# Sorted prefix sums in place of a dense attention, on 14 of 32 samples of a four-layer graph network

## The chip, the cores and the metric

The kernel runs on one core of a Trainium2 chip. The metric is the device time of one execution in microseconds (us), as the median of a few runs; a profile of one further execution is read beside it. Engines: PE (TensorE, matrix products and transposes), DVE (VectorE), ACT (ScalarE), POOL (GpSimd), SP (the queue that issues most DMAs). Each engine runs its own instructions in order and waits on semaphores for the others.

## The reference

32 samples of 512 nodes with 256 features go through four layers, each `x = x + layer(relu(layernorm(x)))`. Layers 0, 2 and 3 are attentions over a given graph `adj`. Layer 1 is a small network with two graph attentions; its first one has no mask, so every node attends to every node:

```python
out = relu(x @ mlp1_w + mlp1_b)            # 512 x 512
h  = out @ W_fc                            # 512 x 512
f1, f2 = h @ a[:512], h @ a[512:]          # one number per node each
e   = leaky_relu(f1[i] + f2[j], 0.2)
att = softmax(e, over j)
out = elu(elu(att @ h)) + residual         # then mlp2_w, and a second, masked attention
```

`leaky_relu` has two straight pieces. For a fixed i, all j with f2[j] above -f1[i] take the weight exp(f1[i] + f2[j]), the others exp(0.2 (f1[i] + f2[j])). Each weight is a factor of i times a factor of j. With the nodes sorted by f2, a row of `att @ h` is a sum over a tail of the sorted nodes with one factor, and over the head with the other.

## The kernel before

Everything is fp32. A sample is held as 4 tiles of 128 nodes or as 512-wide feature-major blocks of 128 partitions. `pipelined` (L597) does not emit instructions at once: the layer functions record them in a `Plan` (L82), which knows for each instruction what it reads and writes (`add`, L124), a cost by engine (`cost`, L333) and which rotating buffer it takes: 60 blocks of 128x512 in SBUF, 8 PSUM banks, small tiles. `order` (L169) then lays all 32 samples out as one list, instruction by instruction: it takes the one that can start first, and among equals the one with the earliest due time, which is the sample's number times PERIOD, less the longest chain of costs behind it, less a hand-set number in URGENT (keys like "p0:0", tile name and layer). STARTS, PACE and LAYERS hold layers back until a set time; OWN, SPARE and KEEP keep buffers for older samples; AHEAD limits how many samples are in flight; SWITCH prices a change of PE between full products, products tiled by columns and products tiled by rows. `issue` (L281) emits the list; all planned instructions have line L297.

The first attention of layer 1 is `first_gat` (L803). PE computes h = o1 W_fc for nodes (mm<-W_fc,o) and the two numbers f1, f2 per node (sd). `largest` finds the largest f2, `on_all` (L756) puts a vector on all partitions by four transposes. DVE makes four 128x512 tiles p of unnormalised weights, one `tensor_scalar` each with two factors per partition and a maximum. `inverse_sums` (L774) adds the four, transposes the total, reduces it and spreads the reciprocals by four more transposes. `weighted` multiplies: 4 feature blocks by 4 node blocks, 16 products of 128x128 by 128x512 (av<-p,v 128*128 128x512). `elu2` (L789) scales by the reciprocals, applies the two elus and adds the residual, on ACT and DVE.

Around it, the other layers do their masked attentions: scores with pairs of 64-row products (sc<-qT,kT, layer 0), products tiled by columns (64 or 32 columns) for av and for sums, exponentials on ACT (p<-R,e; p<-sc), masks on DVE. SP's queue carries R<-rd (a row of scores spread over 128 partitions), the round trip of sums and reciprocals through DRAM (s<-sums, few<-s, s<-few, rc<-s) and x in and out. POOL computes the layernorm's power (rs) and issues accumulating DMAs (p<-p in layer 3, x<-boa in layer 0). The masks of layers 0 and 1 are bf16, that of layer 3 is f32. If tests on the data at the end fail (`tests`, L992, flag go), a slower `general` path (L1086) computes everything again.

Of the kernel before, what the change touches and what calls it, by code (L numbers as in the profile page):

```python
# [12 lines left out]
F32 = mybir.dt.float32  # L13
BF16 = mybir.dt.bfloat16
I32 = mybir.dt.int32
AF = mybir.ActivationFunctionType
# [25 lines left out]

PERIOD = 107.0
STARTS, PACE = (0.0, 4.0, 19.0, 123.0), 101.0
LAYERS = (0.0, 32.0, 34.0, 184.0)

URGENT = {
    "stats:0": -231, "mv:0": -37, "rs:0": -123, "ms:0": -205, "h:0": 11, "pt:0": -750, "hT:0": 14, "mm:0": -216,  # L50
    "sc:0": -122, "p0:0": -65, "total:0": -98, "av:0": 34, "sums:0": -578, "s1:0": 49, "few:0": -6, "s2:0": 16,
    "rc:0": -235, "oT:0": 85, "mv:1": -1, "rs:1": -312, "ms:1": 79, "h:1": -294, "pt:1": -8, "hT:1": 210, "o1:1": 230,
    "sd:1": -3, "v1:1": 496, "nd:1": -243, "ew:1": 150, "p1:1": 192, "total:1": -170, "sm:1": 80, "rs1:1": -271,
    "rc:1": 295, "av:1": -43, "y:1": -155, "e:1": -181, "o2:1": 223, "o3:1": 97, "v2:1": -74, "sd2:1": 230,
    "mn:1": -599, "None:1": 532, "ew2:1": 73, "p2:1": 326, "rs2:1": -12, "u:1": 67, "x:1": 261, "stats:2": 253,
    "mv:2": -2, "ve:2": -111, "rs:2": 9, "ms:2": 327, "h:2": -217, "pt:2": 246, "hT:2": -176, "mm:2": -27,
    "vs:2": -140, "es4:2": -547, "e4:2": 121, "rd:2": -46, "R:2": 10, "p3:2": -509, "av:2": -104, "total:2": -557,
    "sm:2": 273, "r4:2": -73, "ue:2": -350, "x:2": -11, "stats:3": -7, "mv:3": -124, "ve:3": 186, "rs:3": 271,
    "ms:3": -493, "pt:3": 488, "hT:3": -507, "mm:3": -191, "vs:3": -282, "es8:3": 187, "e8:3": -10, "rT:3": -676,
    "rd:3": 450, "R:3": 367, "p3:3": -733, "av:3": -428, "total:3": 545, "sm:3": -50, "sums:3": 213, "raw:3": 11,  # L60
    "s1:3": 84, "s2:3": 121, "rc:3": -208, "oT:3": 42, "None:3": 359, "af:3": 10, "top:3": 409, "ok:3": 38,
    "values:3": -217, "rows:3": 208, "gp:3": -60, "gram:3": -190, "gab:3": 123, "sq:3": -31, "tp:3": -40,
    "res:3": 224,
# [18 lines left out]
class Plan:  # L82
# [9 lines left out]
    HOP, AHEAD = 0.05, 4  # L92

    OWN = dict(block=8, bank=2)
    SPARE = dict(block=2, bank=1)

# [27 lines left out]
    def add(self, attribute, engine, op, args, kw):  # L124
        steps = self.samples[-1]
        out = kw["out"] if "out" in kw else args[0]
        busy, lasts = cost(engine, op, args, kw, out)
        step = self.joined or Step(engine, busy)
        if not step.calls:
            step.layer = self.layer  # L130
            steps.append(step)
        step.calls.append((attribute, op, args, kw))
        step.urgent = URGENT.get(f"{self.kinds.get(out.tensor.name)}:{step.layer}", 0.0)
        step.lasts = step.busy + lasts
        writes = [out] + ([kw["accum_out"]] if "accum_out" in kw else [])
        reads = [v for v in list(args) + list(kw.values()) if isinstance(v, bass.AP) and not any(v is w for w in writes)]
        for ap, writing in [(v, False) for v in reads] + [(v, True) for v in writes]:
            if ap.tensor.name not in self.tile_tag:
                continue
            name, box = ap.tensor.name, extent(ap)  # L140
            if name not in step.touches:
                step.touches.append(name)
            record = self.history.setdefault(name, [])
            for other, obox, owriting in record:
                bank = writing and owriting and step.engine == other.engine == "PE"
                if (writing or owriting) and other is not step and (bank or overlap(box, obox)):
                    if other not in step.before:
                        step.before.append(other)
                        other.after.append(step)
            record.append((step, box, writing))  # L150
        for other in self.gate:
            if other not in step.before:
                step.before.append(other)
                other.after.append(step)
        self.gate = []

    def behind(self, ap):

        self.gate = [step for step, _, writing in self.history[ap.tensor.name] if writing]
# [9 lines left out]
    def order(self):  # L169
# [17 lines left out]
        free["block"][:FILLED] = [FILLED_TO] * FILLED  # L187
# [14 lines left out]
        result, count, mode = [], sum(map(len, self.samples)), "full"  # L202
        oldest = 0

        def slots(step):

            when, taken = 0.0, {}
            for name in step.touches:
# [17 lines left out]
                when = max(when, sorted(free[tag])[n])  # L226
# [3 lines left out]
        while len(result) < count:  # L230
            best = None
            for engine, waiting in open_.items():
                for step in waiting:
                    if step.sample > oldest + self.AHEAD:
                        continue
                    start = max(at[engine], step.ready)
                    if engine == "PE" and step.mode != mode:
                        start = max(start, at[engine] + self.SWITCH[mode])
                    if best is not None and self.key(start, step) >= best[0]:
                        continue  # L240
                    when = slots(step)
                    if when is None:
                        continue
                    start = max(start, when)
                    if best is None or self.key(start, step) < best[0]:
                        best = self.key(start, step), start, step
            assert best is not None, "the buffers do not suffice"
            _, start, step = best
            step.start = start
            open_[step.engine].remove(step)  # L250
# [3 lines left out]
            end = start + step.lasts  # L254
            for name in step.touches:
                tag, s = self.tile_tag[name], step.sample
                if name not in live:
                    live.add(name)
                    free[tag].remove(min(free[tag]))
# [21 lines left out]
    def issue(self, tc, late):  # L281
# [3 lines left out]
        for layer in range(3):  # L285
# [5 lines left out]
            begin = first  # L291
        with tc.manual_schedule():
            for n, step in enumerate(steps):
                for f in at.get(n, ()):
                    f()
                for attribute, op, args, kw in step.calls:
                    getattr(getattr(self.nc, attribute), op)(*args, **kw)  # L297
# [35 lines left out]
def cost(engine, op, args, kw, out):  # L333
# [15 lines left out]
    if engine == "DVE":  # L349
# [5 lines left out]
        return 0.066 + 0.00105 * n + (0.06 if by_pointer else 0.0), 0.085  # L355
    if engine == "POOL":
        if op == "dma_start":
            return 1.1, (5.2 if n == N else 8.0)
        return (1.0 if n < 16 else 0.683), 0.1
    size = 4  # L360
    for _, k in (out.ap if out.tensor.name.startswith(("few", "R", "rc", "x")) else src.ap):
        size *= k
    return 0.4, 3.4 + size / 190e3
# [3 lines left out]
def gnn_stack_kernel(ctx: ExitStack, tc: tile.TileContext, a: dict, out: bass.AP):  # L367
# [45 lines left out]
    go1 = const.tile([1, 1], F32, name="go1")  # L413

    spread = const.tile([P, B], F32, name="spread")
    bq8 = const.tile([P, KD], F32, name="bq8")
# [11 lines left out]
    mask0T = const.tile([P, NT, N], BF16, name="mask0T")  # L428
    mask1T = const.tile([P, NT, N], BF16, name="mask1T")
# [4 lines left out]
    def new_x():  # L434
        return first.tile([P, NT, D], F32, name="x", bufs=5)
# [4 lines left out]
    with prep_stack, tc.manual_schedule():  # L440
# [21 lines left out]
        nc.vector.memset(ones, 1.0)  # L462
        adjf = prep.tile([P, NT, N], F32, name="adjf", bufs=1)
# [133 lines left out]
    def pipelined(stack):  # L597
# [3 lines left out]
        dram = stack.enter_context(tc.tile_pool(name="dram", bufs=6, space=bass.MemoryType.DRAM))  # L601
        q = Plan(nc, PERIOD)
        def block(name):

            return q.tile(big, [P, N], name, BLOCKS, keep=KEEP, tag="block")
# [7 lines left out]
        def small(name, *free):  # L613
            return q.tile(big, [P, *free], name, 4)

# [212 lines left out]

        def second_gat(o3, xt):

            v, sd = q.tile(big, [P, NT, D + 1], "v2", 2), small("sd2", NT, 2)
            for t in range(NT):
                ps = node_major(wh, t, o3, 0, D + 2)
                q.scalar.activation(v[:, t, :D], ps[:, :D], AF.Identity, bias=ones[:, 0:1])
                q.scalar.copy(sd[:, t, :], ps[:, D : D + 2])
            q.vector.memset(v[:, :, D : D + 1], 1.0)
# [13 lines left out]
            for t in range(0, NT, 2):  # L850
                e, u, avs, rs = block("e"), block("u"), [], small("rs2", 2, 2)
                for i in range(2):
                    av = bank("av")
                    avs.append(av)
                    for j in range(NT):
                        q.tensor.matmul(
                            av[:, : D + 1], p[j][:, col(t + i)], v[:, j, :], start=(j == 0), stop=(j == NT - 1)
# [23 lines left out]
        def layer1(xt):  # L881
# [4 lines left out]
            o2 = first_gat(o1)  # L886
# [5 lines left out]
        def separable(xt, w, nh, mask, bars):  # L892
# [13 lines left out]
            rT = q.tile(big, [P, P], "rT", 4, tag="turned")  # L906
            q.scalar.copy(rT[: NT * nh, :], pt[: NT * nh, :P])
            rd = q.tile(dram, [H3, N], "rd", 6)
# [83 lines left out]
        def tests():  # L992
# [8 lines left out]
            for t in range(NT):  # L1001
                ai, af = q.tile(big, [P, N], "ai", BLOCKS, keep=KEEP, tag="block", dtype=I32), block("af")
# [56 lines left out]
        for i in range(B):  # L1059
            q.begin()  # L1060
            q.sample, q.left = i, B - i
            xt = q.adopt(new_x() if i else x0, "x", 5)
# [9 lines left out]
            lambda n: big.tile([P, N], F32, tag="block", name=n, bufs=BLOCKS),  # L1072
# [3 lines left out]
        with tc.manual_schedule():  # L1076
# [6 lines left out]
            nc.vector.tensor_tensor(go1, go1, narrow[:1, :], op=ALU.mult)  # L1083
            nc.vector.tensor_copy(go, go1)
# [413 lines left out]
```

## Time and profile before

| | us |
|---|---|
| median of 3 runs | 3901.18 (3900.81 to 3904.83) |
| profiled execution | 3905.73 |
| its span, first to last instruction | 3903.9 |
| PE, DVE, ACT, POOL busy | 3824.9, 3292.2, 2837.1, 519.1 |
| PE on the 16 dense products of 32 samples (1024 records) | 457.6 |
| DMA moved | 292.65 MB, 75 GB/s |

Busy time is the union of an engine's instructions. A matmul in fp32 stands as two records. Records of matmuls overlap, as matmuls are pipelined: the mean length of one is more than the time that it takes up on the engine, which is the distance from its start to the start of the next. Lines of a group show: line, engine, operation, out<-in by tile names, shapes, count, then busy time and mean length, and the idle time before. Lines of waits show who waited for whom, the total in us, how often, and the longest.

### The profile page before, as it was taken

Reading aid. Unit: us, or ns where it says so; the run is one execution under the profiler, and the core shown is the slowest. Engines: PE = TensorE matmul, PEld = TensorE weight load, DVE = VectorE, ACT = ScalarE, POOL = GpSimd, SP = SyncE. Lnnn points to the kernel's source line nnn. Section 1 sums busy time; section 2 is a strip of 40 time slices with the busy share of each in tenths; the row PEclk is TensorE's granted clock in tenths of the full one; section 3 lists DMA queues with packets and bytes.
Section 4 is the critical chain, followed back from the end, with each engine's and each line's share of the span. In section 5 each row is a group of like instructions: output and inputs, shape, how many; then the busy total and the mean of one; then the engine's idle time right before and its main releaser. Section 6 shows DMA issues by size and latency. Waiting matters only on the chain.

```text
span 3903.9 us, 53766 instructions
## 1 busy us (share of the span) xinstructions
PE 3824.9 (98%) x17400; PEld 2230.5 (57%) x17400; DVE 3292.2 (84%) x7177; ACT 2837.1 (73%) x6128; POOL 519.1 (13%) x530
## 2 busy tenths in 40 slices
PE   8999999999999999999999999999999999999996
PEld 4555565555566555566565556565655555655643
DVE  5578988888988888988889988889888889888896
ACT  4567777777777767777677777677777777776784
POOL 0001110111110111110111111111101111101110
PEclk9999999999999999999999999999999999999998
DMA  3012331323332333332333323333323333314241
GB/s 100 19 48 61 88 93 52 92 61 82 88 84 59 93 61 82 87 76 67 82 63 89 89 66 78 81 63 88 93 58 85 70 73 88 88 55 94 46 110 48
DMA packets 217623, 292.65 MB, mean 75 GB/s; under 512 B 49915, under 2 KB 103422, under 8 KB 217334
## 3 DMA queue, kind: packets, MB, share of 16 engines
q0 software_dynamic: 68864, 111.18, 16.5%
q1 hardware_dynamic: 148196, 177.69, 14.6%
q8 instruction: 140, 2.29, 0.3%
q14 instruction: 149, 1.22, 0.1%
q10 hardware_dynamic: 274, 0.26, 0.0%
HBM read 158.79 MB, written 19.10 MB: 46 GB/s over the span
## 4 chain that ended last, share of the span: by engine, by line
PE 85%; ACT 8%; DVE 3%; issue 2%; DMA 2%; POOL 0%; SPq 0%; DVEq 0%; ACTq 0%; POOLq 0%
PE mm L297 43%; PE av L297 31%; PE pt L297 6%; ACT p L297 6%; PE sm L297 3%; DVE p L297 2%; PE sc L297 1%; DMA p<-p 1%; ACT h L297 1%; DVE total L297 1%; POOL rs L297 0%; DMA rc<-s 0%; DVE x L297 0%; DMA s<-few 0%; DVE rc L297 0%
## 5 line engine op out<-in xcount | busy, mean ns | idle before, releaser
L297 ACT ACTIVATE p<-R,e 128x512 f32<-128x512 f32 x1536 | 1001.5, 716 | 82.5 <-DVE total L297 75.6
L297 DVE SCALAR_TENSOR_TENSOR p<-p,e,mask3T 128x512 f32<-128x512 f32 x1024 | 715.0, 746 | 12.9 <-ACT p L297 12.9
L297 PE MATMUL av<-p,v 128*64 128x512 f32 (+1 forms) x2048 | 697.7, 597 | 6.6 <-ACT v L297 5.4
L297 DVE TENSOR_TENSOR total<-total,p 128x512 f32<-128x512 f32 x808 | 511.3, 686 | 0.1
L297 PE MATMUL av<-p,vs 128*32 128x512 f32 (+1 forms) x3072 | 497.9, 596 | 5.9 <-DVE p L297 5.9
L297 POOL TENSOR_TENSOR rs<-ve,mhalf 128x4 f32<-128x4 f32 x128 | 155.5, 1220 | 2367.8 <-DVE few L297 858.5
L297 POOL DMA_DIRECT2D p<-p x360 | 342.9, 1314 | 934.3 <-PE av L297 790.4
L297 PE MATMUL mm<-W_fc,o 128*128 128x256 f32 (+1 forms) x2048 | 459.5, 380 | 0.4 <-ACT o L297 0.4
L297 PEld LDWEIGHTS av<-p,v 128*64 128x64 f32 (+1 forms) x2048 | 257.6, 163 | 334.5 <-issue 278.1
L297 PEld LDWEIGHTS mm<-W_fc,o 128*128 128x128 f32 x2048 | 384.9, 190 | 83.3 <-issue 22.7
L297 DVE SCALAR_TENSOR_TENSOR p<-p,e,mask1T 128x512 f32<-128x512 f32 x512 | 352.8, 746 | 10.3 <-ACT p L297 10.1
L297 DVE TENSOR_TENSOR p<-p,mask0T 128x512 f32<-128x512 f32 x512 | 317.8, 686 | 13.9 <-ACT p L297 13.9
L297 ACT ACTIVATE h<-x,ms,rs 128x256 f32<-128x256 f32 x512 | 271.4, 593 | 69.9 <-DVE ms L297 69.8
L297 PEld LDWEIGHTS av<-p,vs 128*32 128x32 f32 (+1 forms) x3072 | 138.6, 119 | 310.0 <-issue 263.1
L297 DVE TENSOR_TENSOR total<-p,p 128x512 f32<-128x512 f32 x404 | 267.4, 690 | 39.0 <-PE av L297 22.6
L297 ACT ACTIVATE p<-sc 128x512 f32<-128x512 f32 x512 | 254.4, 673 | 3.7 <-PE sc L297 1.1
L297 PE MATMUL mm<-w,hT 128*128 128x272 f32 (+1 forms) x1024 | 253.5, 396 | 1.3 <-ACT hT L297 1.3
L297 PE MATMUL av<-v,p 128*128 128x257 f32 x1024 | 232.6, 380 | 2.7 <-ACT o L297 1.4
L297 PE MATMUL mm<-o,mlp_w 128*128 128x512 f32 x512 | 230.3, 593 | 2.1 <-DVE o L297 2.1
L297 PE MATMUL mm<-hT,mlp_w 128*128 128x512 f32 x512 | 230.9, 593 | 1.0 <-ACT hT L297 1.0
L297 PE MATMUL sc<-qT,kT 64*128 64x512 f32 x1024 | 228.9, 596 | 0.0
L297 ACT ACTIVATE e<-av,ones,rs 128x256 f32<-128x256 f32 x128 | 65.6, 562 | 220.8 <-PE av L297 108.6
(187 smaller groups left out, 5783.1 us busy)
## 6 DMA issues: line engine op xcount, KB each, us to landing
R<-rd SPq DMA_DIRECT2D x384, 256.0 KB
p<-p POOLq DMA_DIRECT2D x360, 256.0 KB, 4.9
x<-in_x_dram SPq DMA_DIRECT2D x32, 512.0 KB
x<-boa POOLq DMA_DIRECT2D x32, 512.0 KB, 6.5
rc<-s SPq DMA_DIRECT2D x128, 128.0 KB
out_dram<-x SPq DMA_DIRECT2D x32, 512.0 KB
rc<-s SPq DMA_DIRECT2D x248, 64.0 KB
s<-sums SPq DMA_DIRECT2D x94, 8.0 KB
```

The lines of the kernel that those rows point to most:

```text
L297: getattr(getattr(self.nc, attribute), op)(*args, **kw)
```

## The change

1. `sorted_gat` takes the place of `first_gat` on samples 1, 3, 5, ... 27 (14 of 32).
   - The W_fc products are the same; the two halves of h and the numbers f1, f2 of a node go side by side into one row of 514 (tile v1).
   - Ranks: f2 is spread over all partitions by four transposes into one PSUM bank; ACT takes eight passes of the sign of a difference, with the sum of each pass (sg): four rank the node's own f2 (at[0]), four count how many f2 lie below -f1 (at[1]).
   - POOL scatters the four tiles of rows into a DRAM tensor `order`, each row to its rank; SP loads the sorted keys (ds1) and the sorted rows (v1s).
   - ab holds the two factors of each sorted node. Within blocks of 64 sorted nodes, triangular matrices times ab (tile w1) turn a product into prefix and suffix sums: eight 64-row products in pairs (av<-v1s,w1), copied by ACT (tab) and written by SP to a DRAM tensor `table`, with the sums of the weights themselves in 16 further columns (sums1).
   - For every node, POOL gathers two rows of the table (g1, u1) at the places computed from at[1] (pick). The whole blocks further on come from a product of 16 rows (av<-tot,wt), four side by side.
   - DVE adds the parts and scales, ACT applies the elus in node-major form, 16 transposes (pt<-ident,u) bring the result back to feature-major, and the residual is added.
2. The planner: DMAs now take a modelled time on one shared channel (`transfer`, SETUP, NOTICE), and each of SP and POOL has 8 queue slots (LANES); buffers are taken in the order in which they were freed; OWN for blocks 8 to 16, AHEAD 4 to 6; PERIOD, STARTS, PACE, LAYERS and all of URGENT have new numbers.
3. The masks of layers 0 and 1 are one byte per element; blocks are 514 wide; x has 7 buffers in two pools instead of 5.
4. A test that no two keys of a sorted sample are equal (ranks, NO_TIES) joins the flag go.

The core of the diff:

```diff
-PERIOD = 107.0
-STARTS, PACE = (0.0, 4.0, 19.0, 123.0), 101.0
-LAYERS = (0.0, 32.0, 34.0, 184.0)
+SORTED = tuple(range(1, 29, 2))
+PERIOD = 118.0
+STARTS, PACE = (0.0, 0.0, 17.0, 112.0), 99.0
+LAYERS = (0.0, 26.0, 73.0, 214.0)
...
-    HOP, AHEAD = 0.05, 4
-    OWN = dict(block=8, bank=2)
+    HOP, AHEAD = 0.05, 6
+    OWN = dict(block=16, bank=2)
+    SETUP, NOTICE, LANES = 1.4, 0.5, 8
...
+                    if step.transfer:
+                        start = max(start, landed[engine][0])
...
+            if step.transfer:
+                moved = max(moved, start + self.SETUP) + step.transfer
+                end = max(end, moved + self.NOTICE)
+                landed[step.engine] = landed[step.engine][1:] + [end]
...
+        def sorted_gat(o1):
+            rows, ab, nd = [wide("v1") for _ in range(NT)], small("ab", 2, NT), small("nd1", 3)
...
+            pt = bank("pt")
+            for t in range(NT):
+                q.tensor.transpose(pt[:, col(t)], rows[t][:, 2 * D + 1 :].to_broadcast([P, P]), ident)
...
+            for i, scale in enumerate((-1.0, 1.0)):
+                for t in range(NT):
+                    q.scalar.activation(
+                        w, pt, AF.Sign, bias=rows[t][:, 2 * D + 1 - i : 2 * D + 2 - i], scale=scale,
+                        accum_out=sg[:, i, t : t + 1],
+                    )
+                q.vector.tensor_scalar(
+                    at[:, i, :], sg[:, i, :], scale * 0.5, (N - 1 + i) * 0.5, op0=ALU.mult, op1=ALU.add
+                )
...
+            for t in range(NT):
+                q.gpsimd.indirect_dma_start(
+                    out=whole(order), out_offset=bass.IndirectOffsetOnAxis(ap=at[:, 0, t : t + 1].bitcast(U32), axis=0),
+                    in_=rows[t], in_offset=None, bounds_check=N - 1, oob_is_err=False,
+                )
+            ds_ = small("ds1", NT)
+            q.sync.dma_start(ds_, T(order[:, 2 * D + 1 :], "(t p) c -> p (t c)", p=P))
+            put = blocks("v1s", NT)
+            for t in range(NT):
+                q.sync.dma_start(put[t], order[t * P : (t + 1) * P, : 2 * D])
+            q.scalar.activation(ab[:, 0, :], ds_, AF.Exp, bias=nd[:, 2:3], scale=ALPHA)
+            q.scalar.activation(ab[:, 1, :], ds_, AF.Exp, bias=nd[:, 1:2])
...
+            for s in range(2):
+                q.tensor.matmul(sm[:, s * 8 : s * 8 + 8], tri2[:, s, :], T(ab, "p i t -> p (i t)"), start=True, stop=False)
+                q.tensor.matmul(sm[:, s * 8 : s * 8 + 8], ones, T(past, "p i t -> p (i t)"), start=False, stop=True)
...
+            for t in range(NT):
+                tt = [bank("av"), bank("av")]
+                with q.unit("rows", 0.86):
+                    for s in range(2):
+                        r = slice(s * HALF, (s + 1) * HALF)
+                        q.tensor.matmul(tt[s], w[r, col(t)], put[t][r, :], start=True, stop=True)
+                for s in range(2):
+                    b = block("tab")
+                    q.scalar.copy(b, tt[s])
+                    r = (2 * t + s) * P + 1
+                    q.sync.dma_start(table[r : r + P, : 2 * D], b)
...
+            for t in range(NT):
+                q.sync.dma_start(
+                    tot[32 * t : 32 * t + 16, :],
+                    of(LINE, [(P - 1) * LINE, 2], [P * LINE, 8], [1, 2 * D]),
+                )
+            for t in range(NT):
+                g.append(wide("g1")[:, :ROW])
+                u.append(wide("u1")[:, :ROW])
+                for i, b in enumerate((g[t], u[t])):
+                    q.gpsimd.indirect_dma_start(
+                        out=b, out_offset=None, in_=whole(table), bounds_check=2 * N + 1, oob_is_err=True,
+                        in_offset=bass.IndirectOffsetOnAxis(ap=pick[:, i, t : t + 1].bitcast(U32), axis=0),
+                    )
+            behind = [bank("av") for _ in range(NT)]
+            with q.unit("rows", 0.86):
+                for t in range(NT):
+                    r = slice(32 * t, 32 * t + 16)
+                    q.tensor.matmul(behind[t], wt[r, :], tot[r, :], start=True, stop=True)
+            for t in range(NT):
+                e, f, h = block("e"), u[t][:, : 2 * D], g[t][:, : 2 * D]
...
+                q.vector.scalar_tensor_tensor(h, h, ew[:, 0, t : t + 1], behind[t], op0=ALU.mult, op1=ALU.add)
+                q.vector.tensor_tensor(f, f, h, op=ALU.add)
+                q.vector.reciprocal(rs[:, 0, t : t + 1], u[t][:, 2 * D :])
+                q.vector.tensor_scalar(rs[:, 1, t : t + 1], rs[:, 0, t : t + 1], -1.0, None, op0=ALU.mult)
+                q.scalar.activation(e, f, AF.Relu, bias=ones[:, 0:1], scale=rs[:, 1, t : t + 1])
+                q.scalar.activation(e, e, AF.Exp, scale=-1.0)
+                q.scalar.activation(e, e, AF.Exp, bias=mone)
+                q.vector.scalar_tensor_tensor(f, f, rs[:, 0, t : t + 1], e, op0=ALU.mult, op1=ALU.max)
+            o2 = blocks("o2", KH)
+            for m in range(KH):
+                pt = bank("pt")
+                for t in range(NT):
+                    q.tensor.transpose(pt[:, col(t)], u[t][:, col(m)], ident)
+                q.vector.tensor_tensor(o2[m], pt, o1[m], op=ALU.add)
+            return o2
...
-            o2 = first_gat(o1)
+            o2 = (sorted_gat if q.sample in SORTED else first_gat)(o1)
```

A memset of one element (tile filler) stands between each two scatters on POOL.

## The prediction

> **What bounds the kernel now.** I read the page's engine sums first, then the chain that ended last, then one steady stretch, then the order of single TensorE groups in the timeline.
>
> ```profile
> span 3903.9 us, 53766 instructions
> ...
> PE 3824.9 (98%) x17400; PEld 2230.5 (57%) x17400; DVE 3292.2 (84%) x7177; ACT 2837.1 (73%) x6128; POOL 519.1 (13%) x530
> ...
> PE 85%; ACT 8%; DVE 3%; issue 2%; DMA 2%; POOL 0%; SPq 0%; DVEq 0%; ACTq 0%; POOLq 0%
> ```
>
> PE is busy 98% of the span and is 85% of the chain; DMA is 2% of it. The timeline shows the transpose pt<-ident,mx of one layer at 612.4 us and of the next sample at 730.0: a sample takes 117.6 us, two take 235.2, and one such stretch reads:
>
> ```profile
> 493.50:728.70 235.20, 233.37 (x1065) 136.25 (x1064) 204.66 (x441) 175.07 (x379) 33.56 (x34) 1.00 0.33 77
> ```
>
> The columns are window, length, then busy PE, PEld, DVE, ACT, POOL, the granted clock, DMA share, GB/s. PE 233.4 of 235.2: what takes PE time away shortens the sample, so long as nothing arrives late. The price of a PE instruction is its distance to the next start, not its length, as matmuls are pipelined:
>
> ```profile
> 747.57 1.08 PE L297 MATMUL mm<-w,hT 128*128 128x272 f32 x4
> 748.58 7.14 PE L297 MATMUL sc<-qT,kT 64*128 64x512 f32 x32
> 755.65 0.28 PE L297 MATMUL pt<-ident,es 128*32 128x128 f32 x1
> ...
> 1505.07 3.62 PE L297 MATMUL av<-p,vs 128*32 128x512 f32 x32
> 1508.62 0.65 PE L297 MATMUL pt<-ident,ew 128*128 128x128 f32 x4
> ...
> 1515.97 0.60 PE L297 MATMUL sm<-ident,total 128*128 128x128 f32 x4
> 1516.41 2.76 PE L297 MATMUL mm<-wvT,hT 128*128 128x256 f32 x12
> ...
> 1519.44 10.46 PE L297 MATMUL av<-p,v 128*128 128x512 f32 x24
> 1529.74 1.03 PE L297 MATMUL mm<-wvT,hT 128*128 128x256 f32 x4
> ```
>
> An fp32 matmul is two records. The dense product: 10.30 us for 12, so 0.858 each. A transpose: 0.44/4 = 0.11. Pairs on 64 rows run side by side: 7.07 us for 8 pairs, 0.884 a pair with the change of mode at its end (7.07 - 8 x 0.858 = 0.21). Quartets on 32 columns: 3.55/4 = 0.888 (0.12 for leaving that mode). Leaving full mode: 1.01 - 4 x 0.229 = 0.09. Tiny ones: L540 128x1, 1.8 us busy for 8, 0.225.
>
> **The change on PE, per sorted sample.** Removed: 16 dense products x 0.858 = 13.73, and 12 transposes (ew 4, total 4, rs 4) x 0.11 = 1.32; together 15.05. Added: 4 pairs on 64 rows (the block sums), 4 x 0.858 = 3.43; one quartet on 16 rows (the sums behind a block), 0.86; 21 transposes x 0.11 = 2.31; 4 tiny products, 0.90; together 7.50. In the built order two samples change modes 35 times where there were 24 (full 14 for 12, columns 14 for 10, rows 7 for 2): 2 x 0.09 + 4 x 0.12 + 5 x 0.21 = 1.71. Net 15.05 - 7.50 - 1.71 = **5.8 us less per sorted sample, 82 for 14**. The W_fc products and all other layers are the same in number. As a control, the same prices over the two whole PE orders, mode changes with them, give 3746 and 3664 us, again 82 apart; so filling and draining the pipeline bring no other PE work. The few memsets and selects added ahead of the loop fall into the first microseconds, where DVE waits for adj (5.1 us): nothing. The quartet has no row on 16 rows: at best the column quartet's 0.86, at worst four in series, 3.43, +2.6 x 14 = 36 us. I take 0.86, as both shapes of tiling in the trace (pairs, column quartets) run side by side.
>
> **Other engines, per sorted sample.** DVE loses the maxima (4 x 0.553), the totals (2.06), y, o<-y, o<-o (12 x 0.687), the reduction 0.685 and small ones: 13.8. It gains four 512-wide operations for each of 4 tiles (g x ew + sums, u + g, u x rs max e, o<-pt, at 0.69 to 0.75: 11.5), the product with tri 0.69, and about 40 of 0.15 to 0.16: 18.6. Net +4.9, so 209.6 of about 230 a pair, 91%. ACT loses 6.3 (four relus, v, r and rc copies), gains 8 ranking passes of 512 (p<-R is 0.65), 8 copies of 0.58, 8 v copies with a bias at 0.49 and dearer relus: 19.4. Net +13, so 188 a pair, 82%. Both stay under PE. The masks turn from bf16 to one byte: the f32 mask3T and the bf16 mask1T rows both have 746 ns, so I cost it at nothing; 0.06 us either way on 1152 uses is 69 us of DVE, hidden behind PE while DVE is not the bound. The built ACT order has the same seven table loads as before, so the new sign function brings none.
>
> DMA: 1.05 MB of scatters, as much loaded back, 2.2 MB of table written, 2.2 read: 6.4 MB, 90 MB in all, half by POOL. At the page's rates (q0 16.5% for 111.18 MB, q1 14.6% for 177.69 MB) that is 6.7% and 3.7% of the engines' time on 31%. No bandwidth bound.
>
> **The waits added.** PE is in order, so a late transfer stops it. Three crossings per sorted sample have PE behind them. I added the issue costs above between the two ends in the new PE order; from the third sorted sample on it repeats exactly.
> First, ranks to scatter to sorted keys to the weights ab: 23 us of PE work lie between the transposes of v1 and sm<-ab, but ACT fills nearly all of these itself; from its fourth ranking pass to ab it has 11 p<-R x 0.652, 4 more ranking passes (0.65) and 3 copies (0.587): 11.6 us of cover. Behind ab on ACT stand the last p of layer 2, which PE needs next. The trace shows no scatter; the nearest is POOL's accumulating DMA:
>
> ```profile
> p<-p POOLq DMA_DIRECT2D x360, 256.0 KB, 4.9
> ...
> x<-boa POOLq DMA_DIRECT2D x32, 512.0 KB, 6.5
> ```
>
> Its issue has a median of 1.13 us and its landing 3.2/4.9/10.7 (least, median, most). Three issues and three memsets of 0.2 ahead of the last scatter: 4.0. Index arithmetic 0.16. The load of keys: 2.1 (from rd<-rT to R<-rd on SP at 1583.0) to 4.4 (median from few<-s to its reciprocal). Chain: 9.5 at least, 11.2 at the medians, 19.3 at most; so 0 to 7.7 us of stall, or 0 to 108 in all. On POOL the scatters stand ahead of rs of other samples and of p<-p, which would come later by the same.
> Second, block sums to table to gathers to the product with sums behind: 38 us of PE cover against 8 copies with 5 exponentials between (8), a write of 6.5, 8 gather issues (9) and a landing of 4.9: 28. On SP the loads of tot wait for the last table write with s and R loads of others queued behind them; PE's cover is long enough for these 10 us. Third, 20 us from that product to the transposes of u, against some 16 of DVE and ACT work.
> The waits on DMA that the trace has are small, with about five round trips per sample:
>
> ```profile
> ACT v L297 <- DMA p<-p: 17.3, 26, 2.3
> ...
> DVE oT L297 <- DMA rc<-s: 14.8, 4, 9.5
> ...
> ACT p L297 <- DMA R<-rd: 6.9, 3, 6.1
> ```
>
> 39 us in 160 trips is 0.24 each. Three new trips, in a fuller DVE and ACT: I take 1.1 us per sorted sample, **16 in all**; both ends stay in the range.
>
> POOL issues 12 more DMAs, and in the trace DVE's additions total<-total,p have a mean of 674 ns beside a POOL DMA issue (145 of them) and 690 without. [...] By the rows it costs nothing, and I go by the rows.
>
> **Sum.** 3905.7 (profiled execution: span 3903.9 and 1.8 around) - 82 + 16 = 3839.7. The median of the three runs, 3901.2, lies 4.5 lower, so **3835**.
>
> **Rivals.** (a) DVE at 91% and ACT at 82% deliver late in every second sample: PE's own excess now is 235.2 - 229.9 (products and transposes alone) - 2.7 (modes) = 2.6 us a pair; were it 6.2, 50 of the 82 us go, 3869. For it: ACT p is 8% of the chain already. Against: PE has some 20 us of other samples' work at each crossing.
> (b) Slower: the ACT wait at ab. Once the chain of four scatters and the key load passes its 11.6 us of cover by 5.8 (17.4 us long), the gain is gone; at its bound of 19.3 us the time is 3901 - 82 + 108 = 3927. For it: POOL's landings reach 10.7. Against: their median is 4.9.
> (c) The change does not do what it says: the test for equal keys fails, and the general path is run as well; far above the range. Nothing in the profile speaks for it.
>
> **Chances.** Forecast case (waits of 0 to 3 us, 3819 to 3861) 0.58; (a) up to 3893, 0.16; within 0.2%, which is about what a measurement of this kernel can tell from no change, 0.05; (b) 0.18; (c) 0.03. Faster 0.74, same 0.05, slower 0.21. The forecast's own range is 3815 to 3861; the stated one goes from 3810 to 3915, into (b), leaving out about 0.17.
>
> **What would show it.** PE busy near 3745 and a pair of samples near 230 us instead of 235.2; 0.43 us between records of the block sums in pairs, not 0.86; four records of av<-tot within 10 ns of each other; ACT ab waiting on the key load ds1 by no more than about 1 us each; the gathers landed before DVE needs them. Wrong if ACT ab or PE av<-tot wait on DMA for over 80 us together, or if DVE's idle time vanishes.

## The result and the profile after

The changed kernel takes 4010.07 us (median, 4004.91 to 4011.89), the one before 3901.26 beside it: a ratio of 1.0275, with a 95% interval of 1.0257 to 1.0293. It is slower; I had forecast 3835. The forecast is 175 us off, and 109 of these are a loss against before. The profiled execution took 4009.94.

The first lines of the page of the changed kernel, and the first line of its chain:

```profile
span 4007.9 us, 56199 instructions
...
PE 3847.8 (96%) x17529; PEld 2205.4 (55%) x17529; DVE 3301.4 (82%) x7695; ACT 2969.9 (74%) x6506; POOL 944.9 (24%) x748
...
PE 11%; DVE 2%; ACT 1%; issue 0%; DMA 0%; POOL 0%; SPq 0%; DVEq 0%; POOLq 0%
```

PE has 23 us more, not 80 less. DVE has grown by 9 us, ACT by 133. POOL stands out: 944.9 us where it had 519.1. (The chain was followed back over only a small part of this span, so I did not read from it.) A pair of samples in the same view as before, columns as there:

```profile
1623.10:1868.50 245.40, 237.10 (x1080) 135.50 (x1079) 205.20 (x479) 185.56 (x409) 64.64 (x49) 0.99 0.41 101
```

245.4 us where the pair had 235.2, with PE busy for 237.1. My prices for the new order sum to 226.8 (222.4 for products and transposes, 4.4 for changes of mode). So some 18 us of a pair are waiting by these prices: 8.3 us with PE idle, the rest inside "busy" (237.1 against 226.8).

POOL's growth is not only its DMAs. The tile view of rs, the layernorm's power on POOL (least, median and most ns of one); the line of the kernel before first, which I had not looked at, then that of the changed one:

```profile
L297 POOL TENSOR_TENSOR rs<-ve,mhalf x128: 997/1033/2612, 18.9 to 3835.1; 128x4 f32<-128x4 f32 x128
```

```profile
L332 POOL TENSOR_TENSOR rs<-ve,mhalf x128: 1007/1441/15238, 18.8 to 3941.4; 128x4 f32<-128x4 f32 x128
```

The same instruction on 128x4 elements takes 1 us or 15. There are 12 of 15.2 us and 12 of 4.4, one of each per pair (my expectations below say 13 of 4.4). One of the long ones, in the timelines of POOL and of DVE:

```profile
1697.64 15.23 POOL L332 TENSOR_TENSOR rs<-ve,mhalf 128x4 f32<-128x4 f32 x1 [3.89 <-DVE ve L332]
1713.06 1.18 POOL L332 DMA_INDIRECT g<-table,pick  x1 [0.19 <-issue]
...
1722.50 1.01 POOL L332 DMA_INDIRECT u<-table,pick  x1 [0.30 <-issue]
```

```profile
1697.40 0.16 DVE L332 TENSOR_SCALAR ve<-mv 128x4 f32<-128x4 f32 x1
1697.47 4.90 DVE L332 TENSOR_TENSOR p<-p,mask0T 128x512 f32<-128x512 f32 x8
...
1709.51 2.49 DVE L332 TENSOR_TENSOR total<-total,p 128x512 f32<-128x512 f32 x4
1712.90 0.16 DVE L332 SCALAR_TENSOR_TENSOR ms<-mv,rs 128x4 f32<-128x4 f32 x1 [0.90 <-POOL rs L332]
```

DVE writes ve (the layernorm's variances, which rs reads), then runs 24 products and sums with two inputs in SBUF, without a gap, until 1712.00. rs starts with them and ends at 1712.87, 0.87 us after the last: about its own length. So it stood still for the whole run. All of the 24 end so, 0.87 to 0.91 us after a run's end. The eight gathers, 1.3 to 1.5 us apart, stand behind it on POOL, and the first starts 0.19 us after its end. What is late then, among the waits (total us, times, longest); ms is the layernorm's DVE instruction that reads rs, h what ACT makes with it, PEld PE's loading of weights. First the kernel before, then the changed one:

```profile
ACT h L297 <- DVE ms L297: 69.8, 35, 9.6
...
PEld av L297 <- DVE p L297: 46.1, 116, 3.4
...
PE av L297 <- DVE p L297: 8.2, 6, 2.5
```

```profile
PEld av L332 <- DVE p L332: 150.7, 165, 3.4
ACT h L332 <- DVE ms L332: 124.7, 64, 9.6
...
DVE u L332 <- DMA u<-table,pick: 65.3, 11, 6.5
PE av L332 <- DVE p L332: 51.2, 45, 2.5
```

DVE idles for the gathered rows, ACT for ms, and PE for the weights p that both have left undone. (Experiment 4 shows that ACT's wait for ms is no part of what the late gathers cost.) A second loss sits on this. The same pair where PE waits for p, by stretch (the third number from the right is the granted clock):

```profile
1727.00:1730.00 3.00, 1.50 (x6) 0.14 (x2) 3.00 (x10) 1.89 (x9) 2.42 (x4) 1.00 1.05 184
...
1733.00:1735.00 2.00, 1.12 (x10) 0.16 (x8) 2.00 (x4) 1.09 (x2) 0.85 (x2) 0.94 1.11 182
1735.00:1738.00 3.00, 3.00 (x20) 0.80 (x16) 3.00 (x5) 0.00 (x0) 0.77 (x1) 0.50 1.08 179
```

After some 8 us in which PE was about half empty (busy for 4.09 of the 7.70 us from 1727.0), its clock is halved for some 3.4 us. Between 200 and 3600 us the changed kernel has 18 such stretches, which take 30.7 us off the clock; the kernel before has one, 1.7 us. In the 4 us ahead of each of the 18, PE was busy for 1.2 to 2.3 us.

### The profile page after: what moved, and what is told of

It is laid out like the page before. It is cut to its first block, busy times and chain, and to the rows that moved or that the text cites. A ratio compares the mean times of both kernels' runs of the same rounds, so it can differ in the third digit from the quotient of the medians.

```text
span 4007.9 us, 56199 instructions
## 1 busy us (share of the span) xinstructions
PE 3847.8 (96%) x17529; PEld 2205.4 (55%) x17529; DVE 3301.4 (82%) x7695; ACT 2969.9 (74%) x6506; POOL 944.9 (24%) x748
## 5 line engine op out<-in xcount | busy, mean ns | idle before, releaser
L332 ACT ACTIVATE p<-R,e 128x512 f32<-128x512 f32 x1536 | 1027.2, 751 | 15.3 <-DMA R<-rd 11.8
L332 POOL TENSOR_TENSOR rs<-ve,mhalf 128x4 f32<-128x4 f32 x128 | 381.9, 2984 | 1256.6 <-DVE ve L332 821.1
L332 POOL DMA_DIRECT2D p<-p x360 | 318.9, 1093 | 1236.4 <-PE av L332 1059.2
L332 PE MATMUL av<-p,vs 128*32 128x512 f32 (+1 forms) x3072 | 554.4, 601 | 46.4 <-DVE p L332 23.1
L332 PE MATMUL av<-p,v 128*64 128x512 f32 (+1 forms) x1600 | 525.4, 616 | 28.1 <-DVE p L332 28.1
L332 PE MATMUL mm<-W_fc,o 128*128 128x258 f32 (+1 forms) x2048 | 471.1, 380 | 0.0
L332 ACT ACTIVATE h<-x,ms,rs 128x256 f32<-128x256 f32 x512 | 278.4, 611 | 241.4 <-DVE ms L332 124.7
L332 PEld LDWEIGHTS av<-p,v 128*64 128x64 f32 (+1 forms) x1600 | 180.7, 158 | 294.8 <-issue 176.0
L332 PE MATMUL mm<-w,hT 128*128 128x264 f32 (+1 forms) x1024 | 257.7, 396 | 1.6 <-ACT hT L332 1.6
L332 PE MATMUL sc<-qT,kT 64*128 64x512 f32 x1024 | 243.5, 605 | 0.0
L332 PEld LDWEIGHTS mm<-w,hT 128*128 128x128 f32 x1024 | 191.9, 192 | 63.3 <-ACT hT L332 20.0
```

The costliest lines, as they stand in the source:

```text
L332: inst = getattr(getattr(self.nc, attribute), op)(*args, **kw)
```

## The experiments

**Theories.** H1: POOL is shut out while DVE runs instructions with two SBUF inputs one after the other, and what hangs on POOL comes late. H2: the indirect DMAs and their round trips cost the time. H3: byte masks make DVE worse for POOL. H5: DVE or ACT are too full in the sorted samples (my rival (a)), or the new order is bad by itself.

**1. ms directly behind rs.** Then DVE waits out rs and starts no run.

```diff
+        for step in [s for s in steps if s.calls[0][1:2] == ("tensor_tensor",) and s.engine == "POOL"]:
+            use = next(n for n in step.after if n.engine == "DVE")
+            steps.remove(use)
+            steps.insert(steps.index(step) + 1, use)
```

> The changed kernel with one thing moved: of each layernorm, the DVE instruction ms, which reads rs, stands directly behind rs in the list, so that DVE waits out POOL's power instead of running its products first. No work is added or left out. H1 (POOL's rs is shut out while DVE runs TENSOR_TENSORs with two SBUF inputs back to back, and ms, h and the gathers come late): every rs takes 1.0 to 1.3 us, the 12 of 15.2 and 13 of 4.4 us are gone, POOL's rs total falls from 382 to about 135 us, a pair of samples from 245 to about 231, and the time to 3820 to 3870 (DVE idles some 1.1 us 128 times for it). H2 (the indirect DMAs and their transfers are the cost): no less than 3980. H5 (DVE and ACT are too full in the sorted samples): slower than 4010, as DVE gets 140 us of idle time more.

Measured: 3931.39 us, 1.0074 of before (1.0057 to 1.0091). rs: 1006/1346/1492 ns. 79 us come back, against H2, but it stays 60 above what I expected (3870 at most).

> The kernel before with the same move, as a control: its rs instructions mostly take 1.0 to 1.4 us already and three take 2.5. H1: nothing to gain, 3900 to 3960, by what DVE's waits cost. If the move itself speeds up any order (H5 or a mere reordering effect), it falls below 3880.

Measured: 3917.16, 1.0038 (1.0025 to 1.0050). The move itself costs 15 us, so it isn't a better order that helped.

**2. The mask product in another form.**

```diff
+                    if op == "tensor_tensor" and getattr(kw.get("op"), "name", "") == "mult" and any(getattr(getattr(v, "tensor", None), "name", "").startswith("mask0T") for v in args):
+                        op, args, kw = "scalar_tensor_tensor", (args[0], args[1], 1.0, args[2]), dict(op0=ALU.mult, op1=ALU.mult)
```

> The changed kernel with layer 0's mask product issued as scalar_tensor_tensor (times 1.0, times mask) in place of tensor_tensor, in the same places; two SBUF inputs as before. The totals stay tensor_tensor. H1a (any DVE instruction with two SBUF inputs shuts POOL out): rs keeps 15 and 4.4 us, time 4000 to 4030. H1b (only the TENSOR_TENSOR form does; rs took 1.4 us beside p<-p,e,mask in scalar_tensor_tensor form): rs gets through in the first mask product, 1.5 to 3 us, and the time falls to 3820 to 3900. H2: 3980 or more, whatever rs does.

Measured: 4007.97, 1.0266 (1.0244 to 1.0289), rs up to 15.24 us. H1a holds between these two forms, H1b falls.

**3. Small kernels.** The first two measure rs beside runs of DVE by themselves.

> A small kernel by itself that computes none of the reference: POOL's power on 128x4 (and a product, and a DMA issue) while DVE runs 16 instructions of 128x512 of one form back to back, twice for each form: tensor_tensor with f32, byte and bf16 second input, scalar_tensor_tensor with an immediate and with a pointer, tensor_tensor with one PSUM input, tensor_scalar, copy, and no run. H1: power about 1.0 us alone, 10 to 13 us beside tensor_tensor with two SBUF inputs whatever the second's type (a byte mask no worse than bf16, against H3), about 1 us beside one-input and PSUM-input forms; H1b says short beside scalar_tensor_tensor, H1a says long. H2 says that all are near 1 us.

Measured: 1.01 to 1.03 us alone, 1.39 to 1.43 beside tensor_tensors whether the second input is f32, byte or bf16 (against H3), 1.01 beside one PSUM input, 1.26 beside one input. No 10 us: H1 as I had put it did not hold here. The runs differed from the kernel's: all wrote one tile, so each waited 34 ns for the one ahead, where in the kernel a product starts 80 ns before the one ahead ends.

> The small kernel again, computing none of the reference, with one difference: the 16 DVE instructions of a run write 16 different tiles, so that each may start before the one ahead has ended (in the earlier run all wrote one tile, stood 34 ns apart, and POOL's power took 1.4 us beside every form with two SBUF inputs); two forms with one tile as a control; and a plain DMA and a gather issued by POOL beside the runs. H1 as the traces now have it: beside overlapping tensor_tensors and scalar_tensor_tensors with two SBUF inputs the power takes as long as the run, 10 to 11 us or more; beside one PSUM input, one input, or the control 1.0 to 1.5 us. If all stay under 2 us, overlap is not the condition either.

Measured: still 1.39 beside overlapping products. A gather's issue took 1.00 to 1.27 there, 1.01 to 1.09 alone. Overlap by itself is not enough; but here the power began 0.44 us ahead of the first product, in the changed kernel 0.17 us behind one.

**4. Let POOL through, move nothing.**

```diff
...
+                later = [n for n in steps[steps.index(step) :] if n.calls[0][1] == "tensor_tensor" and n.engine == "DVE"]
+                breaks.update(map(id, later[:4]))
...
                     inst = getattr(getattr(self.nc, attribute), op)(*args, **kw)
+                    if id(step) in breaks:
+                        self.nc.vector.tensor_copy(self.gap, args[0][:, 0:1])
```

> The changed kernel, every instruction where it was; behind each of the next four DVE tensor_tensors after the 28 powers (rs) that have four or more of these before their ms, one column of the result just written is copied (112 copies of 128x1 in all), so that DVE has to let the product end before it goes on. Nothing is left out. In the experiment with ms moved, two things changed for these 28: POOL was let through, and ms came 4 to 15 us earlier. This run changes the first alone. If POOL's being shut out is what costs (the gathers queued behind rs on POOL come late): rs falls from 15.2 and 4.4 to under 3 us and the time from 4010 to 3920 to 3960. If the place of ms in DVE's order is what costs: rs falls as well, but the time stays at 3985 to 4015. If rs stays at 15 us, an open slot of some 30 ns behind one instruction is not what lets POOL through.

Measured: 3915.99 us, 1.0035 (1.0024 to 1.0045): 94 us less than the changed kernel, by 112 instructions more. POOL in this run, at the same place:

```profile
1662.60 1.98 POOL L338 TENSOR_TENSOR rs<-ve,mhalf 128x4 f32<-128x4 f32 x1 [3.89 <-DVE ve L338]
1664.76 1.57 POOL L338 DMA_INDIRECT g<-table,pick  x1 [0.19 <-PE pt L338]
1666.64 1.15 POOL L338 DMA_INDIRECT g<-table,pick  x1 [0.30 <-ACT p L338]
```

rs takes 1.98 us (1.98 to 2.02 in all that had 4.4 or 15.2), and the first gather starts 2.2 us after rs began, not 15.4. DVE's wait for the gathered rows (65.3 us) is gone, and the clock's loss is 6.8 us, not 30.7. By the distances between starts on PE, av<-p,vs takes 61.7 us less than in the changed kernel and av<-p,v 30.7: nearly all of the 94. ACT's wait for ms is as it was (125.3 us, 124.7 without the copies), so it is no part of the 94. This shows the main part of H1, that POOL is shut out while DVE runs without a gap, and that the gathers behind it cost the time. H2 falls as the main cause: the order and the DMAs are those of the changed kernel, and only POOL's access was opened. Which instructions of DVE shut POOL out is left to experiment 8.

**5. ms moved for the 28 starved layernorms alone.**

```diff
...
+            if sum(op == "tensor_tensor" and args[0].ap[-1][1] == N for _, op, args, _ in between) > 3:
...
```

> The changed kernel with ms moved directly behind rs, only for the 28 of 128 layernorms that have four or more 512-wide tensor_tensors between rs and ms; the other 100 stay. Nothing is left out. The earlier run moved all 128: 3931 us, with DVE idle about 1 us at each. H1: the 15.2 and 4.4 us are gone as there, and DVE's waits fall from 128 to 28: 3895 to 3930. If the move helped for another reason than the starved 28: 3950 or more.

Measured: 3915.06, 1.0030 (1.0018 to 1.0041), the same as with the copies; the longest rs is 2.66 us. The 28 are the cause of these 94 us, by either cure.

**6. The planner without sorted samples.** `SORTED = ()`, `AHEAD = 4`.

> The changed kernel's planner with its new numbers, byte masks, but no sorted sample: all 32 take the dense form, as before the change. AHEAD is 4 in place of 6, as the buffers do not suffice otherwise. H1: the new order alone does not cost 100 us: 3890 to 3950. H5 (the new order and its numbers are the loss, whatever the attention): 3980 or more.

Measured: 4734.92, 1.2131 (1.2111 to 1.2152). By what I had written this is a point for H5 (3980 or more). But the numbers in STARTS, LAYERS and URGENT are made for the sorted work, so the run can't tell a bad order from an order used for other work; it was badly chosen, and what the new order costs by itself stays open.

**7. The remaining 81 us (3916 against 3835).** Against before, by the distances between starts on PE, the run with the copies takes 40.5 us more on layer 0's scores, 30.2 on its sums, 12.5 on av<-p,vs; the removed products give 204.9. Both of the first wait for DVE at one place in each pair, where the last of the scores stands 2.9 us ahead of the first av (0.52 where nothing is waited for):

```profile
1607.00:1627.00 20.00, 17.27 (x74) 6.50 (x71) 19.86 (x60) 12.20 (x27) 3.46 (x2) 1.00 0.20 55
```

DVE is full (19.86 of 20), PE empty for 2.7. DVE has no gap from 1590.0 to 1635.7: layer 0's 16 mask products and its sums stand among layer 2's 16 mask products and last steps; the sorted work's small instructions take some 2 us of it.

```diff
+                    if op == "activation" and args[2] == AF.Sign and kw["scale"] > 0:
+                        args = (args[0][:, :8], args[1][:, :8], args[2])
```

> The changed kernel with the 112 small copies that let POOL through (3916 us), and the four passes of the sign that count how many keys lie below -f1 narrowed from 512 to 8 columns, so these counts, and with them the places of the gathers, are not the reference's; the order is the same. ACT loses some 4 x 0.5 = 2 us per sorted sample, just ahead of the place where PE waits 2.9 us for layer 0's masked products behind a gapless stretch of DVE. H5a (what is left of the loss is ACT and DVE too full at that place): 20 to 30 us less, 3885 to 3897. If the rest of the loss is spread over the order or lies in the DMA round trips (H2): 3905 to 3916.

Measured: 3917.27, 1.0038 (1.0024 to 1.0053): nothing. These four of ACT's eight ranking passes are not it.

The next run moves ms behind the fourth product and layer 0's masks ahead of planned neighbours:

```diff
...
+            while i > exp and (steps[i].engine != "DVE" or kind(steps[i]) in ("ue", "x", "stats", "mv") and steps[i].layer == 2 or kind(steps[i]) in ("stats", "mv") and steps[i].layer == 3):
+                i -= 1
...
```

> The changed kernel with the 112 small copies, and two moves on DVE, none of work left out: the 28 ms stand behind the fourth product that follows their rs, not behind the whole run; and the products with layer 0's mask stand ahead of statistics and of layer 2's last steps (ue, x, stats, mv) that were planned just before them. H5a: the 2.9 us wait of PE at that place and some of the waits for h go, 3880 to 3905. If DVE's order there is not what PE waits for: 3910 to 3925.

Measured: 3930.20, 1.0073 (1.0057 to 1.0090): 14 us worse. What is put ahead may make something else late; the run changes two things at once and does not show which. Then work was taken out of DVE, in both kernels:

```diff
+                    if op == "tensor_tensor" and any(isinstance(v, bass.AP) and v.tensor.name.startswith("mask0T") for v in args):
+                        args = tuple(v[:, :8] for v in args)
```

> The changed kernel with the 112 small copies (3916 us), and layer 0's mask products on 8 of 512 columns only, so that most of layer 0's weights stay unmasked; order and all else as they were. DVE loses some 0.55 us at each of 512 products, about 8 us per sample. In the run without this, DVE is gapless for 45.7 us of each pair of samples (layer 0's and layer 2's products at once), PE is busy for 17.3 of 20 us there, and against the kernel before PE takes 40.5 us more on layer 0's scores and 30.2 more on its sums, which both wait for DVE. If DVE's stretch is what is left of the loss (the rival that I called (a)): 50 to 80 us less, 3835 to 3865. If it is DMA round trips (H2) or PE's own prices: 3895 to 3916.

> The kernel before with the same narrowing of layer 0's mask products, as a control. DVE is no bound there (PE's waits are 2.6 us of 235.2 a pair): 3865 to 3902, so 0 to 37 us less, clearly less than what the changed kernel gains if DVE's stretch is its cause; as much as there if the narrowing helps any order alike.

Measured: 3872.32, 0.9926 (0.9909 to 0.9942), 44 us less than with the copies; the control 3899.51, 0.9995 (0.9986 to 1.0005), 2 us less. The same cut is worth next to nothing in the order before and 44 us in the new one, so DVE's load by these products is a real part of the rest: just over half, below the 50 to 80 I expected. That it acts at this one place fits the waits, but no run shows it alone. 37 us stay above the forecast; and the stretch is only shortened, as DVE is still without a gap for 35.8 us of each pair.

**8. What shuts POOL out.** The small kernel with the stretch as it stands in the changed kernel.

> The small kernel once more, computing none of the reference, now with the stretch as the changed kernel has it: two products, ve computed between them by DVE, then 16 products of 128x512 in place over 16 tiles, POOL's power starting just after the first of them has begun; fed by ACT (each product waits on a semaphore that is already there) or not; products by scalar_tensor_tensor; not in place; one PSUM input; one input; the first product 64 to 512 columns wide, to shift the phase; and runs of 2, 4, 8. In the two earlier ones the power got through at the first boundary (1.4 us) although products overlapped, unlike in the kernel. If what sets the kernel apart is in the instruction stream, at least one of these forms gives 10 us or more beside two SBUF inputs and none beside one or PSUM; if it is a matter of phase, only some of the widths do; if all stay under 2 us, it takes something that only the whole kernel has, and the condition stays open.

Measured: both lengths, for the same code (first two lines). POOL's rs beside products in place (first three lines, the third with copies by ACT ahead), products into other tiles, and tensor_scalars with one input:

```profile
23.98 1.38 POOL L116 TENSOR_TENSOR rs_in_place_fed<-ve_in_place_fed,mhalf 128x4 f32<-128x4 f32 x1 [23.54 <-DVE ve_in_place_fed L115]
35.03 10.42 POOL L116 TENSOR_TENSOR rs_in_place_fed<-ve_in_place_fed,mhalf 128x4 f32<-128x4 f32 x1 [9.67 <-DVE ve_in_place_fed L115]
47.21 1.38 POOL L116 TENSOR_TENSOR rs_in_place_fed<-ve_in_place_fed,mhalf 128x4 f32<-128x4 f32 x1 [1.76 <-DVE ve_in_place_fed L115]
...
115.19 10.41 POOL L116 TENSOR_TENSOR rs_aside_fed<-ve_aside_fed,mhalf 128x4 f32<-128x4 f32 x1 [9.67 <-DVE ve_aside_fed L115]
...
300.12 6.14 POOL L116 TENSOR_TENSOR rs_single_fed<-ve_single_fed,mhalf 128x4 f32<-128x4 f32 x1 [9.97 <-DVE ve_single_fed L115]
```

5 of 16 runs of two-input products shut rs out to their end (10.41 to 10.42 us), the other 11 let it in at the first boundary (1.38); of the one-input tensor_scalars 2 of 4 (6.14 or 1.29). The 5 are 4 with a byte mask and 1 with f32, and in the kernel before, with bf16 masks, two of the three rs of 2.5 us stood beside layer 0's mask products too; H3 falls.

These runs are not alike in one point. Of each form two ran by themselves and two with 16 copies by ACT ahead. All 7 long ones are among the 10 without the copies; of the 10 with them none is. The 14 runs with a first product of 512 to 96 columns (1.01 to 1.58) and those of 2, 4 and 8 products (1.38) were short, but all had the copies, so they say nothing about the phase. So it is not plain chance, but the copies don't settle it either: without them the same code gave both lengths, and in the changed kernel, where ACT makes what the products read, 26 of the 27 rs that began in a run of four or more two-input products and sums stayed shut out to its end. What decides is open. rs begins 163 to 170 ns after the first product where products with two inputs shut it out and 169 to 173 where not, but 169 to 179 in the long ones of the changed kernel.

Which instructions let POOL in shows better. In the small kernel none of 4 runs shut rs out with a pointer operand (a number per partition beside the two inputs), whose products start 662 ns apart, not 602 (1.44), and none of 4 with a PSUM input (1.01); but only two of each were without the copies. The trace of the changed kernel bears it out: 12 rs that began in runs of four products with a pointer operand (p<-p,e,mask1T) took 1.43 to 1.44 us. The one at 434.5 us stood still through five two-input products and ended 0.87 us after the last, while DVE went on with products with a pointer operand; the one at 424.9 ended 0.91 us after the last, beside x<-mm,x, which has one input in PSUM.

## Why the prediction was wrong, step by step

- **PE's products: right.** The dense products went from 452.5 to 247.6 us (-204.9; with 12 transposes fewer -222), the new ones take 112.6; the net of -110 stands against my -106 ahead of changes of mode. Pairs and quartets run side by side as I had it: the table's pairs cost 0.884 each (49.5 us for 56), a quartet on 16 rows 1.07 (15.0 for 14), not the 3.43 of the bad case:

```profile
1740.48 1.14 PE L332 MATMUL av<-tot,wt 16*128 16x512 f32 x8
```

- **Rival (b): did not happen.** Its chain of 11.2 us "at the medians" takes the load of the keys at 2.1, the lower of its two figures; with 4.4 it is 13.5. All waits for the sorted keys together are about 1 us: "PEld sm <- ACT ab" 1.0, once, and no wait of ab on ds. The scatters' issues had a median of 1.29 us.
- **Rival (c): did not happen.**
- **"I take 1.1 us per sorted sample, 16 in all": this step failed.** By difference, the waits and the slower clock came to some 190 us (175 and 16), not 16. Of the 175, 94 go with the rs that were shut out, 44 with layer 0's mask products on DVE, and 37 are open. I had priced the three crossings by the length of chains between queues, and each POOL instruction at its length in the trace of before. The largest term was in none of the crossings: the gathers wait behind the rs of another sample, and that rs is shut out by a run of DVE. I wrote that the scatters make rs late; it was rs that made the gathers late. One of my signs did fail at this place: the gathers were not landed before DVE needs them (65.3 us of waits).
- **"By the rows it costs nothing, and I go by the rows": the choice behind it.** I tested one direction alone, whether POOL holds DVE up, on the length of DVE's additions beside POOL's DMA issues (674 and 690 ns). DVE was not held up; POOL was. Its row stood in the trace of before, rs 997/1033/2612, and the few of 2.5 us ended 0.9 us after a run of products, as the long ones do. The runs show that DVE instructions with two SBUF inputs can block POOL (15.2 us in the changed kernel); beside a PSUM input rs took 1.01 us. rs was blocked for 24 instructions, not for the one in front. The form counts, too: products with two SBUF inputs and a pointer operand held it up for one instruction at most (1.44 us). The waits came to 15 us at a time on POOL, and to 94 us of the kernel's time.
- **Rival (a): right in kind, wrong in place and size.** I had 50 us, spread over every second sample, 3869. Taking layer 0's mask products out of DVE gives back 44 us, among work of layers 0 and 2 with hardly any of the sorted work in it. DVE's 91% of a pair was an average; where layers 0 and 2 meet it has no gap for 45.7 us.
- **What stays open.** 37 us are left when rs is let through and layer 0's mask products are cut short. The trace of that run still has two waits in each pair: 2.4 us from the last of layer 0's first scores to the start of av (0.52 without a wait), with DVE still without a gap there, and 0.7 to 1.7 from the last av<-p,vs to the product with woT (0.52 without), which follows the round trip of sums through DRAM. The order before has waits of 2.6 us a pair too, so this is not a settled account. No run beat the kernel before with all of its work done; what the products save, the order does not yet use.

My signs for being wrong looked at ab, av<-tot and DVE's idle time. None of these would have named rs; POOL's own instructions should have been in the list.

## What to carry to other kernels

When a change puts work on POOL behind or ahead of small POOL instructions, take the longest, not the median, of those instructions in the trace and see what DVE did meanwhile; a gapless DVE run can hold POOL, and all in its queue, until the run ends (here 15.2 us). A dependent DVE instruction in the run was a cheap way to let POOL in (here copies of 0.15 us). And an engine's share over a pair of samples says little: read it in the stretch where its result is waited for.

## What the runs showed of the hardware

- A 128x4 power on POOL (1.0 us alone) took 15.23 us beside 24 overlapping DVE products and sums with two SBUF inputs, and 1.98 with a dependent copy (0.15 us) behind each of the first four.
- It is not certain: in the changed kernel 26 of 27 rs in such runs were shut out; in a kernel by itself the same stretch gave 1.38 or 10.42 us, and the long ones came only without copies by ACT ahead. One-input tensor_scalars on f32 did it too (6.14).
- Products with a pointer operand or a PSUM input did not: 8 runs by themselves (1.44 and 1.01 us), and 12 rs in runs of products with a pointer operand in the changed kernel (1.43 to 1.44).
- PE's clock was halved for about 3.4 us after short waits, 18 times in the changed kernel between 200 and 3600 us, with PE busy for 1.2 to 2.3 of the 4 us ahead: in one case, at 1652.8 us, it began 0.7 us after a stretch of 2.4 us in which PE was busy for 0.04 us.
